# A graph layer on one Trainium2 core: ScalarE fetches some chunks of edges by columns, and the division moves from VectorE's selections to ScalarE's row copies

## The chip, the cores and the metric

The kernel runs on one core of a Trainium2 chip. The metric is the time of one execution on the device in microseconds; lower is better. A core has TensorE (PE in the profile), VectorE (DVE), ScalarE (ACT), GpSimd (POOL) and the queue engine SyncE (SP), each with its own stream of instructions, and 16 DMA engines that move data between the chip's memory and the core's on-chip memories. An engine runs its instructions in their order; what passes between engines goes by semaphores.

## What is computed

A graph of 12500 nodes and 200000 edges, sorted by destination, with 128 features to a node. Two layers of aggregation over the edges stand between a layer norm and a residual sum. Cut to what matters:

```python
h = maximum(layernorm(x), 0)
w = edge_weight / maximum(segment_sum(edge_weight, dst), EPS)[dst]
feat = relu(h @ W_pool + b_pool)
neigh = segment_max(feat[src] * w[:, None], dst)
rst = h @ W1_self + neigh @ W1_neigh + b1
h1 = relu(rst / maximum(norm(rst), EPS))
neigh2 = segment_sum(h1[src] * w[:, None], dst) / maximum(deg, 1)[:, None]
out = x + relu(h1 @ W2_self + neigh2 @ W2_neigh + b2)
```

The costly parts are the two gathers by `src`, 200000 rows of 512 bytes each, and the two reductions by `dst`, a maximum in layer 1 and a sum in layer 2.

## The kernel before

Edges go in **groups** of 512, 391 of them in each layer, and a group in four **chunks** of 128. For a chunk, `gather` (L525) has POOL issue one indirect DMA that fetches 128 rows of a table in memory by a list of sources, one row to a partition: `feat_d` in layer 1, `h_d` in layer 2. So a group has four such gathers, into one buffer of a ring (`gt`; 11 buffers in layer 2, up to 18 in layer 1).

There is a second way to get a chunk. The tables also lie in on-chip memory, transposed: a node is a column of 128 values (`one_way`, `other_way`). The class `Columns` has an engine copy a chunk column by column, at addresses that it reads into registers. `load` has SP bring the list of 128 addresses; `places_of` (L766) reads 16 of them at a time into the engine's registers (a `TENSOR_LOAD`, which the engine's sequencer does); `fetch` copies the 16 columns of this **burst**. Eight bursts make a chunk. What `Columns` is given decides which groups take part: the chunk `j`, the `first` group and `every`, the distance between them. Its `plan` spreads the eight bursts over the turns ahead of the group: in layer 1 they begin some `every` turns before and end one turn before the group, in layer 2 the span is at most five turns and ends four turns before it. In the kernel before DVE alone does this, for chunk 1: in each 8th group of layer 1 from group 33 on, and in each 3rd of layer 2 from group 13 on. It copies two columns with one instruction (`two_by_two`, L813: one changes its sign on the way). For such a chunk `gather` issues nothing.

**Layer 1** (loop from L1064). The order of each engine's instructions is that of the code, turn by turn; a turn `i` issues the gathers of group `i` and works on groups `i-1` to `i-5` at once. PE transposes the gathered chunks into `pm` (L1099); a chunk that came by columns is multiplied with `W_pool` instead (L1006) and cut by ACT (L1011). DVE multiplies by the edges' weights (L1143), runs a scan that carries the maximum along the edges of one destination (L1114), and takes from each pair of edges the value that may end a destination (L1136, L1139, into `sc`). PE turns `sc` so that pairs stand on partitions (`two_pr`, L1156), ACT copies them (`rows`, L1109). DVE builds a selection for them, `sel`: for each pair a row of 48 numbers, one over the sum of the destination's weights (`invT`) at the place of that destination in the group's window and zero elsewhere (L1125, two instructions of 128x48, one of them between the two that make `sc`). PE multiplies `rows` with `sel` (L1165), and ACT copies the window of 48 nodes into the layer's result (L1045). About every 16 turns four tiles of nodes are finished (`quad1`).

**Layer 2** (loop from L1279). DVE builds the selection with weights in two steps, `places` (L1217) and `weighted` (L1222); PE multiplies each chunk with it (`window_product`, L1229); DVE adds the window to the result (`window_add`, L1234). A chunk that came by columns is turned by PE two turns ahead (`turned`, L1204) and copied back to its buffer by ACT (`back`, L804, which also restores the signs by the scale `signs`).

## Time and profile before

| | |
|---|---|
| median of 3 runs | 4603.24 us (4592.86 to 4608.26) |
| profiled execution | 4644.8 us, its span 4643.0 us |
| layer 1, scan of the first to the last group | 168 to 2361 us |
| layer 2, `places` from there on | 2387 to 4625 us |
| indirect DMAs issued by POOL | 2956 |

The times that follow are from the profiled execution. A row of a group reads: line, engine, operation, what it writes and reads, shapes, count, then busy time in us and mean ns of one, then the idle time of the engine just before these instructions and what ended it. In a row of the timeline the start and the time (us) stand first; instructions of one kind in a row are merged, with their count. "issue" is idle time in which the engine waited for nothing that the profile shows.

### The profile page before, as it was taken

To read this page: it belongs to the slowest core of one execution; us is meant where nothing else is said; L and a number is where in the kernel's file an instruction comes from. 1 tells how busy PE (TensorE), PEld (TensorE's weight loads), DVE (VectorE), ACT (ScalarE), POOL (GpSimd) and SP (SyncE) were. 2 spreads that over 40 slices of the span, in tenths; PEclk is the share of its full clock that TensorE was granted. 3 is DMA by queue.
4 is the path that set the end of the run, shared out by engine and by line. 5 is a ranking of instruction groups with operands and counts; after the bars stand their busy time and mean duration, and the time that the engine had idled before them with its cause. 6 is when DMAs were issued, how large, how long until landed. Compare 5 with 4: busy or idle time off the path is not lost.

```text
span 4643.0 us, 42920 instructions
## 1 busy us (share of the span) xinstructions
PE 2052.8 (44%) x8256; PEld 1667.9 (36%) x8256; DVE 3300.0 (71%) x15295; ACT 489.1 (11%) x1472; POOL 2802.4 (60%) x2973
## 2 busy tenths in 40 slices
PE   4564544444445444454433443433333343334334
PEld 3443333333333333333333433333333333333334
DVE  3678887888888888887755666666666666666665
ACT  3531111111111111111110000000000000000000
POOL 5465665666666666666655655565665665655564
PEclk7755555555555555555555555555555555555555
DMA  4343443433444434444421111111111111111111
GB/s 140 119 116 116 124 118 107 118 118 115 122 122 118 118 116 115 118 123 120 116 70 41 43 51 53 46 49 49 49 46 47 51 47 49 48 49 45 49 49 41
DMA packets 189415, 388.81 MB, mean 84 GB/s; under 512 B 58201, under 2 KB 61570, under 8 KB 189140
## 3 DMA queue, kind: packets, MB, share of 16 engines
q0 software_dynamic: 94592, 193.82, 15.3%
q1 hardware_dynamic: 93812, 191.24, 12.8%
q14 instruction: 204, 1.67, 0.1%
q8 instruction: 71, 1.16, 0.1%
q10 hardware_dynamic: 736, 0.92, 0.1%
HBM read 363.91 MB, written 21.87 MB: 83 GB/s over the span
## 4 chain that ended last, share of the span: by engine, by line
DVE 44%; issue 24%; PE 14%; another core or an unknown queue 11%; DVEq 4%; ACT 1%; POOL 1%; DMA 0%; ACTq 0%; POOLq 0%
DVE gt L813 18%; DVE pm L1114 8%; PE pa L1229 7%; DVE pm L1143 4%; DVEq L766 4%; DVE sel L1125 3%; DVE sc L1139 2%; DVE sc L1136 2%; DVE sq L930 1%; PE pm L1099 1%; PE pn L1165 1%; POOL gt L525 1%; DVE place L1217 1%; PE two_pr L1156 1%
## 5 line engine op out<-in xcount | busy, mean ns | idle before, releaser
L813 DVE SCALAR_TENSOR_TENSOR gt<-ends,way 128x2 f32<-128x2 f32 x10560 | 1590.7, 216 | 724.7 <-issue 704.9
L525 POOL DMA_INDIRECT gt<-h_d,srcT x1426 | 1349.9, 947 | 883.2 <-PE pa L1229 409.6
L525 POOL DMA_INDIRECT gt<-feat_d,srcT x1263 | 1197.0, 948 | 668.8 <-issue 337.4
L1229 PE MATMUL pa<-s,gt 128*128 128x24 f32 x3102 | 717.8, 385 | 1268.8 <-issue 1107.8
L1229 PEld LDWEIGHTS pa<-s,gt 128*128 128x128 f32 x3102 | 693.5, 328 | 1349.3 <-issue 1235.9
L1114 DVE TENSOR_TENSOR_SCAN pm<-kt,pm 128x512 f32<-128x512 bf16 x389 | 499.0, 1283 | 27.1 <-issue 26.6
L1156 PE MATMUL two_pr<-near_ones,sc 128*128 128x128 f32 x782 | 244.5, 413 | 531.1 <-ACT rows L1109 290.0
L1099 PE MATMUL pm<-near_ones,gt 128*128 128x128 f32 (+1 forms) x1263 | 319.8, 401 | 349.6 <-issue 242.1
L1099 PEld LDWEIGHTS pm<-near_ones,gt 128*128 128x128 f32 (+1 forms) x1263 | 221.8, 212 | 405.5 <-issue 282.4
L1156 PEld LDWEIGHTS two_pr<-near_ones,sc 128*128 128x128 f32 x782 | 125.0, 202 | 652.4 <-ACT rows L1109 326.7
L1165 PEld LDWEIGHTS pn<-sel,rows 128*128 128x128 f32 x1564 | 354.5, 312 | 0.2
L1165 PE MATMUL pn<-sel,rows 128*128 128x48 f32 x1564 | 338.7, 362 | 0.0
L1125 DVE TENSOR_SCALAR sel<-cols,lastT,invT 128x48 f32<-128x48 f32 x782 | 246.5, 316 | 108.1 <-remote 89.7
L1143 DVE TENSOR_TENSOR pm<-pm,gs 128x512 f32<-128x512 f32 x390 | 269.9, 692 | 68.9 <-remote 32.3
L1109 ACT ACTIVATE rows<-two_pr 128x256 f32<-128x256 f32 x392 | 149.8, 382 | 1205.4 <-remote 701.9
L804 ACT ACTIVATE gt<-flip,ends 128x128 f32<-128x128 f32 x125 | 45.9, 367 | 1746.2 <-PE flip L1204 792.7
L1136 DVE COPY sc<-pm 128x256 f32<-128x256 f32 x391 | 162.5, 416 | 72.1 <-remote 47.1
L1139 DVE COPY_PREDICATED sc<-kt,pm 128x256 f32<-128x256 int16 x389 | 168.4, 433 | 45.0 <-DVE sel L1125 31.3
L525 POOL DMA_INDIRECT w2T<-feat_d,srcT x98 | 92.7, 946 | 88.6 <-DVE raw_mv L539 35.7
L1217 DVE TENSOR_TENSOR place<-place,locT 128x96 f32<-128x96 f32 x391 | 101.6, 260 | 61.1 <-issue 47.2
L1222 DVE TENSOR_TENSOR s<-place,w2T 128x96 f32<-128x96 f32 x391 | 97.8, 250 | 27.2 <-issue 26.3
L1234 DVE TENSOR_TENSOR way<-pa,way 128x41 f32 x391 | 75.6, 193 | 54.7 <-PE pa L1229 22.6
(305 smaller groups left out, 1963.4 us busy)
## 6 DMA issues: line engine op xcount, KB each, us to landing
gs<-in_edge_weight SPq DMA_DIRECT2D x389, 256.0 KB
kt<-keep_d SPq DMA_DIRECT2D x97, 512.0 KB
gt<-h_d,srcT POOLq DMA_INDIRECT x1426
gt<-feat_d,srcT POOLq DMA_INDIRECT x1263
feat_d<-fr SPq DMA_DIRECT2D x24, 256.0 KB
xr<-in_x SPq DMA_DIRECT2D x24, 256.0 KB
out<-o SPq DMA_DIRECT2D x24, 256.0 KB
h_d<-sq SPq DMA_DIRECT2D x23, 256.0 KB
```

Of the source, the lines that this page charges most:

```text
L525: nc.gpsimd.indirect_dma_start(out=gt[:k, j, :], out_offset=None, in_=table_d[:, :], in_offset=bass.IndirectOffsetOnAxis(ap=srcT[:k, t, j, ...
L766: _, self.held[g, r] = nc.values_load_multi_w_load_instructions(self.lists[self.place[g]][:, r:r + BURST], [self.engine], min_val=self.at, ...
L813: nc.vector.scalar_tensor_tensor(slot[:, r + e:r + e + 2], zero_high, columns_read[e], columns_read[e + 1].to_broadcast([P, 2]), op0=OP.su ...
L1099: nc.tensor.transpose(pms[i][:, j * P:j * P + k], gt[:k, j, :], ident[:k, :k])
L1114: nc.vector.tensor_tensor_scan(pm[:, :ne], kt[:, :ne], pm[:, :ne], carry, op0=OP.add, op1=OP.max)
L1125: nc.vector.tensor_scalar(part, cols[:k, 1, :], lastT[:k, t, j, r:r + 1], invT[:k, t, j, r:r + 1], op0=OP.is_equal, op1=OP.mult)
L1136: nc.vector.tensor_copy(sc[:, :ne // 2], two[:, :, 1])
L1139: nc.vector.copy_predicated(sc[:, :ne // 2], new[:, :, 1], two[:, :, 0])
L1143: nc.vector.tensor_tensor(pms[i][:, :n], rows[:, :n], ws.pop(i)[:, :n], OP.mult)
L1156: nc.tensor.transpose(prs[g][:k, j, :], sc[:, j * P:j * P + k], ident)
L1165: nc.tensor.matmul(pas[g], rows[:k, j, :], sel[:k, j, :], start=j == 0, stop=j == len(chunks) - 1)
L1229: nc.tensor.matmul(pas[g][:, PART_AT[j]:PART_AT[j] + PART], gt[:k, j, :], s[:k, j, :], start=j == len(chunks) - 1, stop=j == 0, skip_group ...
```

## The change

A second `Columns` is added in each layer, for ACT and chunk 2: each 4.25th group of layer 1 from group 30 on (the group is 30 plus the whole part of a multiple of 4.25), each 3.5th of layer 2 from group 14 on. ACT copies one column with one instruction (`one_by_one`, by `by_scalar`, L804), with the sign as it is. These are 85 chunks in layer 1 and 107 in layer 2; POOL issues 192 indirect DMAs less. In layer 1 the multiplication and the cut follow as for DVE's chunks, the cut in one instruction; in layer 2 the turn by PE and the copy back by ACT, with no scale.

The selection becomes one instruction of 128x96 on DVE that writes one or zero; the division is done by ACT in the row copies, which become two of 128x128 with `invT` as their scale.

```diff
--- before.py
+++ after.py
@@ -997,7 +997,8 @@
 
         pms, scs, sels, prs, rws, pas = ({} for _ in range(6))
         bycol = []
-        for k, engine, copy, j, every, first in ((0, mybir.EngineType.DVE, two_by_two, 1, 8, FIRST + 16),):
+        for k, engine, copy, j, every, first in ((0, mybir.EngineType.DVE, two_by_two, 1, 8, FIRST + 16),
+                                                 (1, mybir.EngineType.Activation, one_by_one, 2, 4.25, FIRST + 13)):
 
             def slot(g, j=j):
                 return buffer(g, True)[:, j, :]
@@ -1105,36 +1106,33 @@
                 t, r, ne, chunks = pairs_of(g)
                 rws[g] = wk.tile([P, Q // 2, D], F32, name="rows", bufs=2)
                 pr = prs.pop(g)
-                for j, k in (((slice(0, Q // 2), P),) if ne == G else chunks):
-                    nc.scalar.activation(rws[g][:k, j, :], pr[:k, j, :], AF.Copy)
+                for j, k in chunks:
+                    nc.scalar.activation(rws[g][:k, j, :], pr[:k, j, :], AF.Copy, scale=invT[:k, t, j, r:r + 1])
             g = due(1)
             if g is not None:
                 ne = edges_of(g)[2]
                 kt, pm = kts.pop(g), pms.pop(g)
                 nc.vector.tensor_tensor_scan(pm[:, :ne], kt[:, :ne], pm[:, :ne], carry,
                                              op0=OP.add, op1=OP.max)
-            picks = []
-            if due(3) is not None:
-                t, r, _, chunks = pairs_of(due(3))
+
+            def pick():
+                t, r, ne, chunks = pairs_of(due(3))
+                n, k = len(chunks), chunks[-1][1]
                 sel = sels[due(3)] = wk.tile([P, Q // 2, LW], F32, name="sel", bufs=2)
-                picks = [(sel[:k, j, :], k, t, j, r) for j, k in chunks]
-
-            def pick():
-                if picks:
-                    part, k, t, j, r = picks.pop(0)
-                    nc.vector.tensor_scalar(part, cols[:k, 1, :], lastT[:k, t, j, r:r + 1],
-                                            invT[:k, t, j, r:r + 1], op0=OP.is_equal, op1=OP.mult)
+                for a, b, k in ((0, n, P),) if ne == G else [(j, j + 1, k) for j, k in chunks]:
+                    nc.vector.tensor_tensor(sel[:k, a:b, :], cols[:k, 1:2, :].to_broadcast([k, b - a, LW]),
+                                            lastT[:k, t, a:b, r:r + 1].to_broadcast([k, b - a, LW]), OP.is_equal)
 
             for c in bycol[:1]:
                 c.ahead()
-            pick()
+            if due(3) is not None:
+                pick()
             if g is not None:
                 carry = pm[:, ne - 1:ne]
                 sc = scs[g] = wk.tile([P, G // 2], F32, name="sc", bufs=2)
                 two = pm[:, :ne].rearrange("p (c two) -> p c two", two=2)
                 new = kt[:, :ne].bitcast(I16).rearrange("p (c two) -> p c two", two=2)
                 nc.vector.tensor_copy(sc[:, :ne // 2], two[:, :, 1])
-            pick()
             if g is not None:
                 nc.vector.copy_predicated(sc[:, :ne // 2], new[:, :, 1], two[:, :, 0])
             if i < NG:
@@ -1195,7 +1193,8 @@
             nc.vector.tensor_copy(iota[:, j, :], cols[:, 0, at:at + PART])
 
         bycol = []
-        for k, engine, copy, j, every, first in ((0, mybir.EngineType.DVE, two_by_two, 1, 3, 13),):
+        for k, engine, copy, j, every, first in ((0, mybir.EngineType.DVE, two_by_two, 1, 3, 13),
+                                                 (1, mybir.EngineType.Activation, one_by_one, 2, 3.5, 14)):
 
             def slot(g, j=j):
                 return buffer(g, False)[:, j, :]
```

Three places show what this does to the order. First ACT in layer 1, two turns in a row, before; `way` is the layer's result, `pn` the product with the selection:

```order
L1109 ACTIVATE rows<-two_pr 128x256
L1045 ISA
L1045 ACTIVATE way_66<-pn 128x48
L1109 ACTIVATE rows<-two_pr 128x256
L1045 ISA
L1045 ACTIVATE way_66<-pn 128x48
```

And two turns in which it fetches, now (`listed` are the lists of addresses, `way_65` the table, `gt` the buffer):

```order
L804 ACTIVATE gt_102<-way_65 128x1 x16
L766 TENSOR_LOAD listed
L804 ACTIVATE gt_102<-way_65 128x1 x16
L766 TENSOR_LOAD listed
L1110 ACTIVATE rows<-two_pr,invT 128x128 x2
L1046 ISA
L1046 ACTIVATE way_66<-pn 128x48
L804 ACTIVATE gt_102<-way_65 128x1 x16
L766 TENSOR_LOAD listed
L804 ACTIVATE gt_102<-way_65 128x1 x16
L766 TENSOR_LOAD listed
L1110 ACTIVATE rows<-two_pr,invT 128x128 x2
```

Between a turn's row copies and the next there are now two bursts of 16 copies with their loads, and the row copy is in two parts.

Second DVE in layer 1, around the selection, before (its own burst of columns at the end of a turn, the scan, the load for the next burst):

```order
L813 SCALAR_TENSOR_TENSOR gt_107<-ends,way_65 128x2 x8
L1114 SCALAR_TENSOR_TENSOR pm<-kt,pm 128x512
L766 TENSOR_LOAD listed
L1125 TENSOR_SCALAR sel<-cols,lastT,invT 128x48
L1136 COPY sc<-pm 128x256
L1125 TENSOR_SCALAR sel<-cols,lastT,invT 128x48
L1139 COPY_PREDICATED sc<-kt,pm 128x256
L1143 TENSOR_TENSOR pm<-pm,gs 128x512
```

and now:

```order
L813 SCALAR_TENSOR_TENSOR gt_106<-ends,way_65 128x2 x8
L1115 SCALAR_TENSOR_TENSOR pm<-kt,pm 128x512
L766 TENSOR_LOAD listed
L1123 TENSOR_TENSOR sel<-cols,lastT 128x96
L1135 COPY sc<-pm 128x256
L1137 COPY_PREDICATED sc<-kt,pm 128x256
L1141 TENSOR_TENSOR pm<-pm,gs 128x512
```

One instruction is gone, and the two that make `sc` follow each other directly.

Third ACT in layer 2. Before, it had only the copies back from `flip` (and one copy for every four tiles of nodes):

```order
L804 ACTIVATE gt_101<-flip,ends 128x128
L804 ACTIVATE gt_104<-flip,ends 128x128
L804 ACTIVATE gt_107<-flip,ends 128x128
L946 ACTIVATE oT_43860<-pn,b_col 128x512
L804 ACTIVATE gt_99<-flip,ends 128x128
```

Now there are bursts between them, in most turns two, in some three:

```order
L804 ACTIVATE gt_99<-way_66 128x1 x16
L766 TENSOR_LOAD listed
L804 ACTIVATE gt_103<-way_66 128x1 x16
L766 TENSOR_LOAD listed
L804 ACTIVATE gt_107<-flip,ends 128x128
L804 ACTIVATE gt_107<-flip 128x128
L804 ACTIVATE gt_103<-way_66 128x1 x16
L766 TENSOR_LOAD listed
L804 ACTIVATE gt_103<-way_66 128x1 x16
L766 TENSOR_LOAD listed
```

The copy back with `ends` is that of DVE's chunk, the one without that of ACT's own; both stand behind the bursts that were issued before them.

## Prediction

> **What bounds the kernel now.** I read the shares and the chain of waits on the page first.
>
> ```profile
> span 4643.0 us, 42920 instructions
> PE 2052.8 (44%) x8256; PEld 1667.9 (36%) x8256; DVE 3300.0 (71%) x15295; ACT 489.1 (11%) x1472; POOL 2802.4 (60%) x2973
> DVE 44%; issue 24%; PE 14%; another core or an unknown queue 11%; DVEq 4%; ACT 1%; POOL 1%; DMA 0%; ACTq 0%; POOLq 0%
> ```
>
> DVE is the busiest engine and leads the chain; ACT, which the change loads, is busy for 11%. Averages over two layers say little, so I took a stretch of 1800 us from each by the view of windows: all engines (first two rows), then the scan of L1114, once a group of layer 1, then `places` (L1217), once a group of layer 2.
>
> ```profile
> 500.00:2300.00 1800.00, 857.51 (x3512) 668.58 (x3512) 1468.99 (x4741) 246.46 (x838) 1159.55 (x1225) 0.55 0.40 118
> 2600.00:4400.00 1800.00, 712.63 (x2816) 612.82 (x2816) 1171.18 (x7622) 51.80 (x125) 1080.40 (x1143) 0.50 0.17 48
> 500.00:2300.00 1800.00, 409.57 (x319) 0.55 0.40 118
> 2600.00:4400.00 1800.00, 81.59 (x314) 0.50 0.17 48
> ```
>
> The columns are PE, PEld, DVE, ACT and POOL. A group takes 1800/319 = **5.64 us in layer 1** and 1800/314 = **5.73 us in layer 2**. DVE is busy 4.60 us of a group in layer 1 and 3.73 in layer 2. Where the rest of layer 2 goes stands in the groups by line of the same stretch:
>
> ```profile
> L525 POOL DMA_INDIRECT gt<-h_d,srcT x1143 | 1081.5, 946 | 722.8 <-PE pa L1229 360.2 <-issue 315.7 <-remote 27.1
> L813 DVE SCALAR_TENSOR_TENSOR gt<-ends,way 128x2 f32<-128x2 f32 x6654 | 1012.4, 216 | 527.4 <-issue 510.2
> L1217 DVE TENSOR_TENSOR place<-place,locT 128x96 f32<-128x96 f32 x314 | 81.6, 260 | 49.1 <-issue 38.4 <-DVE way L1234 10.5
> ```
>
> Before L813, the column fetch, DVE stood idle for 527 us, 1.68 us a group, and waited for nobody: "issue". POOL's largest wait is for PE, that is, for a buffer to come free. So layer 2 is held by DVE and not by the gathers. But the timeline shows that the two are tied:
>
> ```profile
> 3187.11 0.94 POOL L525 DMA_INDIRECT gt<-h_d,srcT  x1 [2.56 <-PE pa L1229]
> ...
> 3204.62 0.95 POOL L525 DMA_INDIRECT gt<-h_d,srcT  x1 [0.30 <-issue]
> 3210.67 0.95 POOL L525 DMA_INDIRECT gt<-h_d,srcT  x1 [5.11 <-PE pa L1229]
> 3211.92 0.95 POOL L525 DMA_INDIRECT gt<-h_d,srcT  x1 [0.30 <-issue]
> ```
>
> ```profile
> 3197.78 0.48 DVE L813 SCALAR_TENSOR_TENSOR gt<-ends,way 128x2 f32<-128x2 f32 x3 [1.07 <-issue]
> ...
> 3204.16 0.22 DVE L813 SCALAR_TENSOR_TENSOR gt<-ends,way 128x2 f32<-128x2 f32 x1 [1.07 <-issue]
> ...
> 3215.35 1.17 DVE L813 SCALAR_TENSOR_TENSOR gt<-ends,way 128x2 f32<-128x2 f32 x8 [0.17 <-issue]
> ...
> 3216.82 1.14 DVE L813 SCALAR_TENSOR_TENSOR gt<-ends,way 128x2 f32<-128x2 f32 x8
> ```
>
> Between 3187.11 and 3204.62 the gathers follow each other at 1.25 us without a pause. After some ten microseconds of that, DVE starts one or a few pairs of columns between gaps of about 1.1 us, and goes back to bursts of eight once POOL has run out of buffers. In a good stretch a burst takes 3216.82 − 3215.35 = **1.47 us**; over the 1800 us it took (1012.4 + 527.4)/6654 × 8 = **1.85 us**, 1.26 times as much. At 1.47 a group of layer 2 would need 8 × 1.47/3 = 3.92 us of DVE for columns and (1171.18 − 1012.4)/314 = 0.51 for the rest, 4.4 in all. POOL needs (4 − 1/3) × 1.25 = 4.58. The two are about equally fast, and POOL, whenever DVE falls behind, runs ahead until its buffers are full.
>
> In layer 1 POOL needs (4 − 1/8) × 1.25 = 4.84 of 5.64 us, and DVE's 4.60 carries the chain together with waits that the profile can't name.
>
> **The change, part by part.** *One selection.* In layer 1 DVE now does this in each group:
>
> ```profile
> 1206.45 0.28 DVE L1125 TENSOR_SCALAR sel<-cols,lastT,invT 128x48 f32<-128x48 f32 x1
> 1206.65 0.41 DVE L1136 COPY sc<-pm 128x256 f32<-128x256 f32 x1
> 1206.98 0.37 DVE L1125 TENSOR_SCALAR sel<-cols,lastT,invT 128x48 f32<-128x48 f32 x1
> 1207.20 0.43 DVE L1139 COPY_PREDICATED sc<-kt,pm 128x256 f32<-128x256 int16 x1
> 1207.53 0.69 DVE L1143 TENSOR_TENSOR pm<-pm,gs 128x512 f32<-128x512 f32 x1
> ```
>
> From the first selection to the predicated copy it is 0.75 us. The single selection of 128x96 has no row; L1217, of that size and kind, takes 0.260, some 0.17 of it before the next can start. The copy then takes 0.33 (its step to the second selection now) to 0.41 (if the predicated copy must wait for its end). So 0.50 to 0.58 remain, and 0.17 to 0.25 us a group go; I take 0.17. For 391 groups that is 66 us of DVE's time.
>
> *The division goes to ACT.* One row copy becomes two with a scale that is read from SBUF. What ACT's instructions cost, by the groups (rows 1 to 3 and 5), the timeline (row 4) and the view of one line (row 6):
>
> ```profile
> L1109 ACT ACTIVATE rows<-two_pr 128x256 f32<-128x256 f32 x392 | 149.8, 382 | 1205.4 <-remote 701.9 <-PE pn L1165 203.2 <-issue 189.9
> L1045 ACT ACTIVATE way<-pn 128x48 f32 x391 | 81.6, 209 | 129.6 <-issue 66.1 <-PE pn L911 41.5 <-PE pn L1165 7.7
> L804 ACT ACTIVATE gt<-flip,ends 128x128 f32<-128x128 f32 x125 | 45.9, 367 | 1746.2 <-PE flip L1204 792.7 <-PE pa L1229 569.2 <-remote 199.6
> 245.61 1.63 ACT L555 ACTIVATE lastT<-lastT,raw_off,raw_rstd 128x128 f32<-128x128 f32 x4
> L555 ACT ACTIVATE lastT<-lastT,raw_off,raw_rstd 128x128 f32<-128x128 f32 x4 | 1.6, 481 | 0.0
> L766 DVEq TENSOR_LOAD <-listed x1360: 1093/1099/1684, 315.6 to 4605.1; - x195
> ```
>
> 256 and 48 columns differ by 173 ns, 0.83 ns a column, so an ACT copy with plain scale starts from 169 ns. Four copies of 481 ns in a row take 1.63 us: each starts 383 ns after the last, an overlap of 98. L804 has one scale from SBUF: 367 − 98 = 0.27 us a step. Two such against one of 0.28 add 0.26 us a group to ACT.
>
> *ScalarE's columns.* 85 chunks in layer 1 and 107 in layer 2 are now copied column by column: 128 copies of 128x1 and eight loads of 16 addresses each. No row has such a copy. From below it is 169 + 1 − 98 = 72 ns a step, all loads hidden: 1.15 us a burst of 16. From above, DVE's step for its pairs, (1.14 − 0.216)/7 = 132 ns, and the load, which holds the sequencer for 1.10 us (the last row above), not hidden at all: 3.2 us. L555 reads SBUF and not PSUM: 481 less 107 for its columns and 2 × 92 for its two operands from SBUF (92 = 367 − 107 − 168) is 190, a step of 93 ns. That is the value I take. In DVE's burst of 1.47 us, eight steps of 132 leave 0.42 of the load's 1.10 open, so about five queued instructions cover the rest; five of ACT's cover 0.47 and leave 0.63. A burst is then 16 × 0.093 + 0.63 = **2.12 us** and a chunk 17.0.
>
> ACT in a group: layer 1 has 246.46/319 = 0.77 now, 0.26 for the rows, 0.06 for the chunk's relu, 17.0/4.25 = 4.00: **5.1 us**. Layer 2 has 51.80/314 = 0.17, 0.08 for the copy back, 17.0/3.5 = 4.86: **5.1 us**. Both lie a tenth under today's group, and ACT becomes the fullest engine of both layers. It isn't free: behind each burst wait the row copies and the window copy of layer 1, and DVE's chunk, coming back from its flip, in layer 2; PE waits for these and DVE for PE.
>
> *The gathers.* 192 of 2956 fall away: POOL needs (4 − 1/8 − 1/4.25) × 1.25 = 4.55 in layer 1 and (4 − 1/3 − 1/3.5) × 1.25 = 4.23 in layer 2. SP has 192 more short loads of lists in its queue, half a KB each, two buffers to a list, loaded two turns ahead of use; PE has 107 more flips of 0.45 us in layer 2, where it is idle most of the time. I cost both at nothing. That holds as long as ACT keeps up: a late ACT keeps a list's buffer, and the weights of layer 1 queue behind it on SP.
>
> **The sum.** POOL, at 4.23 against 5.1, will now wait a little in most groups of layer 2 instead of running for 18 us without a pause, and it is after such runs that DVE's gaps came. So I expect a group to approach its fullest engine, ACT with 5.1, and leave a third of the distance for waits: 5.30 in layer 1, 5.25 in layer 2. Columns are fetched from turn 25 to 390 and from 7 to 383: 365 × 0.34 + 376 × 0.48 = 124 + 181 = **305 us**. DVE's 66 us are in it. The profiled execution took 4644.8 us (span 4643.0), 0.9% above the median of the runs, 4603.24; the same gain gives **4298 us**.
>
> **A rule against it.** DVE's gaps look like a port that is taken. The Trainium skill, "SBUF — State Buffer", section "Who interferes with whom", has VectorE and GpSimd share one pair of ports: a VectorE instruction with two SBUF inputs, as L813 is, fully blocks against a GpSimd instruction that reads SBUF; ScalarE waits for nobody. The row at 3215.35 speaks against it: eight pairs at full step while gathers follow at 1.25 us. By the rule each gather removed would give DVE its share of the gaps and no more, the second rival's price.
>
> **Rivals.**
>
> 1. *ACT too slow* (the other side). If ACT's bursts stretch as DVE's do, by 1.26, a burst is 2.67 us, a chunk 21.4, and ACT needs 6.13 in layer 1 and 6.35 in layer 2: +0.49 × 365 + 0.62 × 376 = +412, 5015 us. It decides from a burst of 2.4 us on, in both layers: (5.64 − 1.1) × 4.25/8 and (5.73 − 0.25) × 3.5/8. For it: 2.12 is near 2.4, and DVE's gaps have no cause that leaves ACT out. Against: it needs columns that are slow on ACT, of which no row tells. With the upper bound of 3.2 it would be +1200.
> 2. *A share for each gather.* 527 us of gaps at 1143 gathers are 0.46 us a gather; 192 fewer give 88, with DVE's 66 a gain of 154: 4449 us. For it: gaps and gathers come together. Against: at the row of 3215.35 they don't.
> 3. *DVE stays the bound.* POOL waited for buffers already; if fewer gathers change nothing in DVE's gaps, only the selection counts: 4537 us.
> 4. *ACT just eats what DVE gains*: 4603 us.
>
> **How the numbers follow.** Forecast 0.49 (4150 to 4440), rival 1 0.25, rival 2 0.10, rival 3 0.11, rival 4 0.05. Faster by over 0.3% (14 us, about what a measurement can tell here) is 0.49 + 0.10 + 0.11 = 0.70; within 0.05; slower 0.25. The range runs from 4140, layers at 5.1 and a little less, to 4800, which takes in rivals 2 to 4 and half of rival 1; below lie some 0.04, above 0.13.
>
> **What would show it.** L813 on ACT with a step near 93 ns and bursts near 2.1 us; groups of 5.2 to 5.4 us by the scan and by `places`; ACT near 95% busy or in loads; POOL's waits for PE frequent and short; fewer gaps before DVE's L813. A burst over 2.4 us on ACT, or DVE waiting for PE and PE for ACT's rows and flips, would make the prediction wrong on the slow side; unchanged gaps before L813 with POOL waiting longer make rival 3.

## The result, and the profile after

| | before | after |
|---|---|---|
| median | 4600.2 us (4 runs, 4592.86 to 4608.26) | 5248.07 us (4 runs, 5237.06 to 5257.55) |
| profiled execution, its span | 4644.8, 4643.0 us | 5243.78, 5242.0 us |
| layer 1, scan of the first to the last group | 168 to 2361 us | 166 to 2702 us |
| layer 2, `places` from there on | 2387 to 4625 us | 2728 to 5227 us |
| indirect DMAs issued by POOL | 2956 | 2764 |

The ratio is 1.1407 (95% interval 1.1375 to 1.1439): the change makes the kernel **14% slower**, where 4298 us were forecast. Both layers lose, 343 us the first and 261 the second by the table. The runs below went to several chips, and each is set against the kernel before on its own chip, whose time was 4600 to 4656 us on most and 3737 to 3741 on two. One of the slower chips gave 4600.48 us in one series of runs and 4656.38 in a later one, and none was seen in both ranges; so a kind of chip is known here by its time alone. A run given with an interval is the median of 2 to 10 executions, one without is a single execution; the kernel before beside them is a median of 3 to 13 (a single one beside the last run).

The shares and the chain of waits on the page of the changed kernel:

```profile
PE 2034.7 (39%) x8448; PEld 1690.1 (32%) x8448; DVE 3222.4 (61%) x14905; ACT 3256.2 (62%) x26630; POOL 2622.7 (50%) x2781
...
ACT 48%; issue 32%; PE 6%; DVE 5%; ACTq 4%; another core or an unknown queue 3%; POOL 3%; DVEq 0%; DMA 0%; POOLq 0%
```

ACT leads the chain where DVE did, but it is busy for 62%, not 95%, and the second entry of the chain is "issue", time in which an engine waited for nothing that the profile shows. Three groups of the same page show where it lies:

```profile
L804 ACT ACTIVATE gt<-way 128x1 f32 x23168 | 2536.4, 193 | 1457.2 <-issue 1429.3
...
L525 POOL DMA_INDIRECT gt<-h_d,srcT x1319 | 1248.9, 947 | 1243.8 <-PE pa L1228 790.5
L1228 PE MATMUL pa<-s,gt 128*128 128x24 f32 x3102 | 701.5, 373 | 1623.9 <-ACT gt L804 1464.2
```

Before its column copies ACT stood idle for 1457 us, nearly all of it "issue". PE waits for ACT, POOL waits for PE. By the groups of a stretch of 2000 us in each layer (500 to 2500, then 3000 to 5000):

```profile
L804 ACT ACTIVATE gt<-way 128x1 f32 x8425 | 921.1, 196 | 492.2 <-issue 486.6 <-DMA w2T<-feat_d,srcT 0.9
...
L804 ACT ACTIVATE w2T<-way 128x1 f32 x512 | 57.0, 198 | 39.1 <-issue 38.6
```

```profile
L804 ACT ACTIVATE gt<-way 128x1 f32 x11278 | 1232.6, 191 | 691.9 <-issue 686.9
```

Busy and idle time together, a column costs (921.1 + 492.2 + 57.0 + 39.1)/8937 = 169 ns in layer 1 and (1232.6 + 691.9)/11278 = 171 ns in layer 2: bursts of **2.70 and 2.73 us**, above the 2.4 us from which the prediction's first rival decides. DVE in the same two stretches, the rows of its pairs and of the line that runs once a group:

```profile
L1115 DVE TENSOR_TENSOR_SCAN pm<-kt,pm 128x512 f32<-128x512 bf16 x302 | 388.8, 1288 | 0.1
L813 DVE SCALAR_TENSOR_TENSOR gt<-ends,way 128x2 f32<-128x2 f32 x2216 | 314.9, 216 | 1.0 <-issue 1.0
```

```profile
L813 DVE SCALAR_TENSOR_TENSOR gt<-ends,way 128x2 f32<-128x2 f32 x6580 | 985.1, 217 | 506.0 <-issue 490.7
L1216 DVE TENSOR_TENSOR place<-place,locT 128x96 f32<-128x96 f32 x309 | 81.0, 262 | 55.7 <-DVE way L1233 38.2 <-issue 17.3
```

A group takes 2000/302 = **6.62 us** in layer 1 and 2000/309 = **6.47 us** in layer 2 (5.64 and 5.73 before). In layer 1 DVE has no gap before its pairs any more, but it had few before, as this row of the kernel before from 500 to 2300 us shows:

```profile
L813 DVE SCALAR_TENSOR_TENSOR gt<-ends,way 128x2 f32<-128x2 f32 x2376 | 344.5, 213 | 55.3 <-issue 55.2
```

That is 55.3/319 = 0.17 us a group. ACT's gaps in layer 1, (492.2 + 39.1)/302 = 1.76 us a group, are ten times that, so they are more than DVE's gaps handed on. In layer 2 DVE's gaps are what they were, 506.0/6580 = 77 ns a pair against 527.4/6654 = 79, and ACT's came on top.

One such gap from near, in the timeline of layer 2: POOL, then ACT, DVE and PE.

```profile
4100.96 0.94 POOL L525 DMA_INDIRECT gt<-h_d,srcT  x1 [3.44 <-PE pa L1228]
4102.21 0.94 POOL L525 DMA_INDIRECT gt<-h_d,srcT  x1 [0.30 <-issue]
...
4113.46 0.95 POOL L525 DMA_INDIRECT gt<-h_d,srcT  x1 [0.30 <-issue]
```

```profile
4104.39 1.49 ACT L804 ACTIVATE gt<-way 128x1 f32 x15
4106.61 0.30 ACT L804 ACTIVATE gt<-way 128x1 f32 x2 [0.73 <-issue]
4107.33 0.20 ACT L804 ACTIVATE gt<-way 128x1 f32 x1 [0.43 <-issue]
4108.04 0.30 ACT L804 ACTIVATE gt<-way 128x1 f32 x2 [0.50 <-issue]
4108.77 0.20 ACT L804 ACTIVATE gt<-way 128x1 f32 x1 [0.43 <-issue]
4109.49 0.20 ACT L804 ACTIVATE gt<-way 128x1 f32 x1 [0.52 <-issue]
...
4115.15 0.30 ACT L804 ACTIVATE gt<-way 128x1 f32 x2 [1.20 <-issue]
```

```profile
4106.83 1.14 DVE L813 SCALAR_TENSOR_TENSOR gt<-ends,way 128x2 f32<-128x2 f32 x8 [1.00 <-issue]
...
4108.32 1.14 DVE L813 SCALAR_TENSOR_TENSOR gt<-ends,way 128x2 f32<-128x2 f32 x8 [0.17 <-issue]
```

```profile
4120.26 2.33 PE L1228 MATMUL pa<-s,gt 128*128 128x24 f32 x10 [9.02 <-ACT gt L804]
```

POOL begins a run of gathers at 4100.96. ACT still copies 15 columns in 1.49 us, a step of (1.49 − 0.20)/14 = 92 ns, at 4104. From 4106 on it starts one or two columns each 0.7 us, until after the end of the run. DVE goes through full bursts of 1.14 us at the same time. PE then waits 9 us for ACT.

This is the rule and not a chosen case. Call a column copy late if it starts over 0.3 us after the one before it. Counted in the packed trace from 3000 to 5000 us, all 64 runs of gathers at 1.25 us that last 12 us or more have four or more late copies in them or in the 3 us behind them; of the 37 runs that last 3 to 6 us, 8 have. Half of the stretches (four or more late copies, each within 2 us of the next) begin 3.6 to 5.6 us after the first gather of their run.

### The profile page after: what moved, and what is told of

The parts are those of the page before. It is cut to its first block, busy times and chain, and to the rows that moved or that the text cites. A ratio compares the mean times of both kernels' runs of the same rounds, so it can differ in the third digit from the quotient of the medians.

```text
span 5242.0 us, 69992 instructions
## 1 busy us (share of the span) xinstructions
PE 2034.7 (39%) x8448; PEld 1690.1 (32%) x8448; DVE 3222.4 (61%) x14905; ACT 3256.2 (62%) x26630; POOL 2622.7 (50%) x2781
## 3 DMA queue, kind: packets, MB, share of 16 engines
q14 instruction: 411, 3.37, 0.2%
## 4 chain that ended last, share of the span: by engine, by line
ACT 48%; issue 32%; PE 6%; DVE 5%; ACTq 4%; another core or an unknown queue 3%; POOL 3%; DVEq 0%; DMA 0%; POOLq 0%
ACT gt L804 40%; ACTq L766 3%; ACT rows L1110 3%; POOL gt L525 2%; DVE gt L813 2%; ACT w2T L804 1%; PE pn L910 1%; ACT way L1046 1%; PE pa L1228 1%; PE pm L1100 1%; ACT pm L1012 1%; PE pn L911 1%; PE pn L1163 1%; PE two_pr L1154 1%
## 5 line engine op out<-in xcount | busy, mean ns | idle before, releaser
L804 ACT ACTIVATE gt<-way 128x1 f32 x23168 | 2536.4, 193 | 1457.2 <-issue 1429.3
L813 DVE SCALAR_TENSOR_TENSOR gt<-ends,way 128x2 f32<-128x2 f32 x10560 | 1563.5, 217 | 645.1 <-issue 626.0
L525 POOL DMA_INDIRECT gt<-h_d,srcT x1319 | 1248.9, 947 | 1243.8 <-PE pa L1228 790.5
L525 POOL DMA_INDIRECT gt<-feat_d,srcT x1189 | 1128.5, 949 | 1045.0 <-PE pm L1100 676.2
L1228 PE MATMUL pa<-s,gt 128*128 128x24 f32 x3102 | 701.5, 373 | 1623.9 <-ACT gt L804 1464.2
L1100 PE MATMUL pm<-near_ones,gt 128*128 128x128 f32 x1189 | 314.1, 411 | 272.3 <-ACT pm L1012 247.2
L1123 DVE TENSOR_TENSOR sel<-cols,lastT 128x96 f32<-128x96 f32 x392 | 97.0, 248 | 426.1 <-PE pn L1163 370.9
L1100 PEld LDWEIGHTS pm<-near_ones,gt 128*128 128x128 f32 x1189 | 231.4, 232 | 319.9 <-ACT pm L1012 275.9
L1110 ACT ACTIVATE rows<-two_pr,invT 128x128 f32<-128x128 f32 x782 | 245.9, 364 | 68.0 <-issue 38.8
L1046 ACT ACTIVATE way<-pn 128x48 f32 x391 | 84.0, 215 | 103.8 <-PE pn L911 71.2
```

Source lines behind the costliest of these rows:

```text
L525: nc.gpsimd.indirect_dma_start(out=gt[:k, j, :], out_offset=None, in_=table_d[:, :], in_offset=bass.IndirectOffsetOnAxis(ap=srcT[:k, t, j, ...
L804: nc.scalar.activation(out, in_, AF.Copy, **scale)
L813: nc.vector.scalar_tensor_tensor(slot[:, r + e:r + e + 2], zero_high, columns_read[e], columns_read[e + 1].to_broadcast([P, 2]), op0=OP.su ...
L1100: nc.tensor.transpose(pms[i][:, j * P:j * P + k], gt[:k, j, :], ident[:k, :k])
L1110: nc.scalar.activation(rws[g][:k, j, :], pr[:k, j, :], AF.Copy, scale=invT[:k, t, j, r:r + 1])
L1228: nc.tensor.matmul(pas[g][:, PART_AT[j]:PART_AT[j] + PART], gt[:k, j, :], s[:k, j, :], start=j == len(chunks) - 1, stop=j == 0, skip_group ...
```

## Experiments

My theory after this: instructions of ACT and DVE **start late while gathers are in flight**; ACT needs 16 starts for a burst where DVE needs 8, and so it becomes what ends last. The rival: the columns cost ACT too much in any case, or their loads and code hold it up. (Code here is the stream of instructions that an engine is fed.)

### Parts of the change

`e1_sel`, no columns on ACT in either layer (the selection and the row copies alone); `e2_act1`, ACT's columns in layer 1 only; `e3_act2`, in layer 2 only. From the changed kernel:

```diff
-        for k, engine, copy, j, every, first in ((0, mybir.EngineType.DVE, two_by_two, 1, 8, FIRST + 16),
-                                                 (1, mybir.EngineType.Activation, one_by_one, 2, 4.25, FIRST + 13)):
+        for k, engine, copy, j, every, first in ((0, mybir.EngineType.DVE, two_by_two, 1, 8, FIRST + 16),):
...
-        for k, engine, copy, j, every, first in ((0, mybir.EngineType.DVE, two_by_two, 1, 3, 13),
-                                                 (1, mybir.EngineType.Activation, one_by_one, 2, 3.5, 14)):
+        for k, engine, copy, j, every, first in ((0, mybir.EngineType.DVE, two_by_two, 1, 3, 13),):
```

(both for `e1_sel`, the second for `e2_act1`, the first for `e3_act2`). `e5_nogather` is the changed kernel without the gathers of layer 2 from group 200 on; PE there multiplies old rows:

```diff
-                gts[i] = gather(buffer(i, False), h_d, i, besides=bycol)
+                gts[i] = gather(buffer(i, False), h_d, i, besides=bycol) if i < 200 else buffer(i, False)
```

> The kernel before with the one selection and ACT's two scaled row copies alone; no columns on ACT. Theory A (ACT's stream of columns is what costs the time; the selection is a small gain on DVE): layer 1 goes from 5.64 to about 5.47 us a group, layer 2 stays at 5.73, 4530 to 4590 us in all. Theory B (the selection, or the second row copy on ACT, costs part of the loss): layer 1 over 5.7 us a group, over 4620 us.

> The change without ACT's columns in layer 2. Theory A: layer 1 as in the change, 6.6 us a group, layer 2 back at 5.73, about 4950 us. A rival, that the longer program as such slows both layers: layer 2 stays over 6 us a group.

> The change without ACT's columns in layer 1. Theory A: layer 1 at about 5.5 us a group, layer 2 as in the change, 6.5, about 4850 us.

> The change, with all gathers of layer 2 left out from group 200 on (PE works on what the buffers hold from earlier groups); columns on DVE and ACT as before. Theory A1 (ACT's and DVE's starts are slowed while gathers are in flight): from group 200 on no stretches with steps of 0.7 us, ACT's bursts at 1.9 us throughout, a group at 8 x 1.9 / 3.5 + 0.25 = 4.6 us; the first 200 groups as in the change, 6.5. Theory A2 (the instructions themselves come too slowly, whatever POOL does): the stretches stay and a group stays over 6 us. Theory A3 (the loads of addresses): the same as A2, bursts over 2.4 us.

All four ran on a chip where the kernel before took 3737.32 us: 3744.78 (ratio 1.0017, 1.0007 to 1.0027), 3724.46, 3616.26 and 3591.4 us. Three rows of their pages, `e1_sel` first, then two of `e3_act2`:

```profile
L813 DVE SCALAR_TENSOR_TENSOR gt<-ends,way 128x2 f32<-128x2 f32 x10560 | 1519.7, 215 | 239.9 <-issue 217.9
```

```profile
L813 DVE SCALAR_TENSOR_TENSOR gt<-ends,way 128x2 f32<-128x2 f32 x10560 | 1520.8, 215 | 206.9 <-issue 183.3
L804 ACT ACTIVATE gt<-way 128x1 f32 x13696 | 1361.1, 188 | 38.9 <-issue 17.6 <-PE pa L1227 16.2 <-ACT gt L804 1.1
```

Here DVE's gaps are a third (240 us, not 725), and ACT has next to none: (1361.1 + 38.9)/13696 = 102 ns a column, bursts of 1.64 us. And here the columns **gain**: those of layer 2, with the one selection that alone was worth nothing, make 3.2% (3616.26 against 3737.32). `e5_nogather` couldn't test the gathers, since there was no gap before group 200 to take away. Its first 200 groups of layer 2, which are the changed kernel's own, took 4.25 us each, and those without gathers, from 2850 to 3550 us, 700/165 = 4.24.

So I ran both kernels again, unchanged: does the loss go with the chip?

> The change as it is, once more, beside the kernel before. In the four runs just made no stretch of slow starts is left, in kernels with and without ACT's columns. Theory S (the change loses only where instructions start slowly while gathers are in flight, and gains where they don't): without such stretches layer 1 at 4.6 us a group and layer 2 at 4.25, about 3595 us beside 3737, ratio 0.96; with them 5245 beside 4600, ratio 1.14. Theory T (the change loses anyway, the two layers' columns together): slower than before, whatever the stretches.

> The kernel before as it is, for its trace beside that of the change. Theory S: without slow stretches DVE's bursts of columns at 1.47 us throughout, layer 1 at 4.7 and layer 2 at 4.55 us a group, 3737 us; with them 5.64 and 5.73, 4600 us.

This chip was one of the others: 5316.49 us against 4647.38 (1.1454, 1.1427 to 1.1481) and 4647.69 for the kernel before, taken as a run of its own. The loss is there again. There is no run of the whole changed kernel on a chip of the quicker kind; what it would do there rests on its parts.

### What the gathers have to do with it

Four kernels on one chip with the kernel before at 4600.48 us: the changed kernel, the one without gathers from group 200 on, one with narrow gathers there and one with pauses of POOL there. The last two:

```diff
+            nc.gpsimd.indirect_dma_start(
+                out=gt[:k, j, :16], out_offset=None, in_=table_d.rearrange("n (a b) -> (n a) b", b=16)[:, :],
+                in_offset=bass.IndirectOffsetOnAxis(ap=srcT[:k, t, j, r:r + 1], axis=0))
```

```diff
+    idle = rp.tile([P, 2], F32, name="idle")
...
+            if j % 2:
+                for _ in range(4):
+                    nc.gpsimd.memset(idle, 0.0)
             nc.gpsimd.indirect_dma_start(
```

> The changed kernel as it is. Theory S: what it does hangs on whether ACT and DVE get into stretches in which instructions start only every 0.7 us while gathers are in flight. If groups of layer 2 show such stretches here, they last 6.2 to 6.8 us and the run is 5200 to 5350, 13 to 15% above before on the same chip; if there are none (steps of ACT's columns over 0.3 us are under a tenth of their time), groups are 4.2 to 4.6 us and the run is 3570 to 3640, 3 to 5% below before. Theory T (the columns on ACT cost more than they free in any case): above before either way.

> The changed kernel without the gathers of layer 2 from group 200 on (their buffers keep old rows, so the output of these nodes isn't the reference's); what ACT and DVE fetch by columns stays. If the stretches of late starts come from gathers in flight (theory G): groups before 200 as in the changed kernel of the same chip (6.2 to 6.8 us where there are stretches), from 200 on 4.2 to 4.7 us, with hardly a step of ACT's columns over 0.3 us. If they come from the engines' own instruction streams (theory I: ACT's 16 loads and 16 copies a burst, fetched code): 6.0 to 6.8 us on both sides of group 200. On a chip without stretches: 4.2 to 4.3 on both sides, and nothing is told apart.

> The changed kernel with gathers of 16 instead of 128 elements a row in layer 2 from group 200 on (an eighth of the bytes, the same number of gathers and of rows; the rest of each chunk keeps old values, so the output of these nodes isn't the reference's). Theory G1 (what the gathers write, the bytes into SBUF, holds starts back): groups from 200 on fall to 4.2 to 4.8 us. Theory G2 (what POOL does to issue them, once for each row, holds starts back): they stay at 6.0 to 6.8 us where those before 200 are there. Without stretches on this chip: 4.2 to 4.4 on both sides.

> The changed kernel with four small memsets (about 0.5 us by 118 ns each) on POOL ahead of each second gather of layer 2 from group 200 on, so that POOL never issues more than two gathers without a pause; POOL then needs about 5.2 us a group (3.38 gathers of 1.25 us and two pauses). Theory R (stretches come after a long run of gathers without a pause, as runs of 12 to 15 us always had one and runs of 3 to 6 us had one in seven): groups from 200 on fall to 5.2 to 5.6 us. Theory N (only the mean number of gathers in a time counts): they stay at 6.2 to 6.8 us. Without stretches: 4.2 before 200, about 5.2 behind it.

Measured: 5253.37 us (1.1417, 1.1334 to 1.1501), 4818.73, 5253.27 and 5056.55. In the stretch from 4100 to 4750 us, which lies behind group 200 in all four, the groups by line give for ACT's copies, in the order above:

```profile
L804 ACT ACTIVATE gt<-way 128x1 f32 x3651 | 397.8, 190 | 229.3 <-issue 227.6 <-DVE gt L813 0.4
```

```profile
L804 ACT ACTIVATE gt<-way 128x1 f32 x5596 | 556.6, 188 | 7.5 <-issue 5.5
```

```profile
L814 ACT ACTIVATE gt<-way 128x1 f32 x3648 | 398.0, 190 | 230.2 <-issue 228.9
```

```profile
L819 ACT ACTIVATE gt<-way 128x1 f32 x4325 | 471.2, 189 | 148.1 <-issue 141.6 <-ACT gt L819 0.5
```

And for `places`, once a group, the first, second and fourth:

```profile
L1216 DVE TENSOR_TENSOR place<-place,locT 128x96 f32<-128x96 f32 x100 | 26.0, 260 | 15.8 <-DVE way L1233 11.1 <-issue 4.7
```

```profile
L1216 DVE TENSOR_TENSOR place<-place,locT 128x96 f32<-128x96 f32 x154 | 40.3, 262 | 24.6 <-DVE way L1233 23.6 <-issue 1.0
```

```profile
L1231 DVE TENSOR_TENSOR place<-place,locT 128x96 f32<-128x96 f32 x119 | 31.0, 261 | 19.5 <-DVE way L1248 13.0 <-issue 6.5
```

Without gathers the idle time before ACT's copies falls from 229 us to 7.5, a column costs (556.6 + 7.5)/5596 = 101 ns, and a group goes from 650/100 = 6.5 us to 650/154 = **4.22 us**. Ahead of group 200 the same execution, `s_nogather` from 3000 to 3900 us, is like the changed kernel:

```profile
L804 ACT ACTIVATE gt<-way 128x1 f32 x5050 | 552.2, 190 | 313.7 <-issue 310.0 <-ACT gt L804 0.2
L1216 DVE TENSOR_TENSOR place<-place,locT 128x96 f32<-128x96 f32 x140 | 36.4, 260 | 25.8 <-DVE way L1233 18.8 <-issue 6.8
```

There a column costs (552.2 + 313.7)/5050 = 171 ns and a group takes 900/140 = 6.43 us. The loads, the copies and the code of ACT are the same on both sides of group 200, so by themselves they don't hold it up. With gathers of an eighth of the bytes nothing changes at all (3648 copies, 230.2 us): it is not the bytes but something that a gather of 128 rows brings with it at either width. With the pauses the idle time falls to 148 us and the group to 650/119 = 5.46 us. POOL got more gathers through than without pauses:

```profile
L525 POOL DMA_INDIRECT gt<-h_d,srcT x338 | 319.8, 946 | 334.9 <-PE pa L1228 245.0 <-issue 88.3 <-PE flip L1203 0.9
```

```profile
L541 POOL DMA_INDIRECT gt<-h_d,srcT x403 | 381.7, 947 | 154.5 <-issue 76.0 <-PE pa L1243 49.0 <-ACT gt L819 6.0
```

403 gathers against 338 in the same 650 us, with fewer late starts: it isn't the mean number of gathers that counts, but how they follow one another. On the quicker kind of chip that isn't enough either: in `e3_act2` POOL's gathers of layer 2 follow each other at 1.25 us nearly throughout (95% of the steps from 2100 to 3500 us are at most 1.26), and ACT has the 38.9 us of gaps shown above.

The packets in the traces tell where no delay is seen. `e1_sel`, from 2100 to 3500 us, and `v_sel` below, from 2700 to 4400, are the same kernel on the two kinds of chip. On both, 95% of the gathers have their first packet within 1.67 us of the issue, and the last packet of 95% ends within 2.53 us in the first and 2.42 in the second: the gathers are no slower where ACT and DVE start late, and no queue of them builds up. The other suspect is the code, which a DMA queue of its own brings ("q14 instruction" on the page of the changed kernel: 411 packets, 3.37 MB, nearly all of 8 KB). A packet of it takes 0.40 us at the median and never over 0.97, and none is under way from 4104.90 to 4122.91 us, where the stretch shown above lies. So late code isn't seen either, though nothing here excludes a delay behind that queue.

### Is it a bound, and is the rest of the change free?

On a chip with the kernel before at 4649.7 us: the pauses in both layers of the changed kernel; the same in the kernel before; the changed kernel with half of ACT's chunks; and the selection alone once more.

```diff
-                                                 (1, mybir.EngineType.Activation, one_by_one, 2, 4.25, FIRST + 13)):
+                                                 (1, mybir.EngineType.Activation, one_by_one, 2, 8.5, FIRST + 13)):
...
-                                                 (1, mybir.EngineType.Activation, one_by_one, 2, 3.5, 14)):
+                                                 (1, mybir.EngineType.Activation, one_by_one, 2, 7, 14)):
```

> The changed kernel with the pauses (four memsets of POOL, 0.43 us, ahead of each second gather) in both layers from their first gathered group on. If starts are held back after long runs of gathers (theory R; the pause took layer 2 from 6.5 to 5.45 us a group), layer 1 falls too, to 5.4 to 5.9 us by POOL's 3.64 gathers of 1.25 and two pauses, and the run is 4420 to 4620 where before has 4600: about as fast as before or up to 4% faster. If layer 1's loss has another cause than layer 2's: layer 1 stays at 6.6 us, the run at 4800 to 4900. Where a chip shows no stretches: 3950 to 4200, above the 3595 that the changed kernel should have there.

> The kernel before with the same pauses in both layers. POOL then needs about 5.5 us a group in layer 1 (3.88 gathers) and 5.3 in layer 2 (3.67). Theory R: DVE's late starts shrink, groups 5.4 to 5.7 us, the run 4430 to 4620. If pauses only help where ACT is what ends last: groups 5.8 to 6.3, the run 4700 to 4950.

> The changed kernel with half of ACT's chunks (each 8.5th group of layer 1, each 7th of layer 2). If what the change loses is that ACT's bursts of 2.8 us end last (theory L: bursts of a chunk of 22.5 us in 3.5 groups make 6.4 us a group), ACT has 3.2 us a group and is no longer last: groups 5.5 to 5.8 us, the run 4480 to 4660, near before. If the columns lose by something that each of them adds (theory E: half the columns, half the loss): groups 6.0 to 6.2, the run 4880 to 4960.

> The kernel before with one selection a group and the dividing row copies alone, no columns on ACT. Where there are stretches of late starts: 4540 to 4640 (my term: 66 us less on DVE, of which late starts may leave nothing; on another chip, without stretches, it was 1.0017 of before). If the selection itself loses where there are stretches: over 4700.

`v_half` took 4673.16 us, 0.5% above before. Half of the columns would have lost some 320 us if each cost its share; they lost 23. So the loss is a **bound**: ACT's late bursts end last when there are enough of them (ACT's share of the chain is 12% here and 48% in the full change). ACT's late starts are still there, but it also waits for PE, which the full change hardly knew:

```profile
L804 ACT ACTIVATE gt<-way 128x1 f32 x11648 | 1331.2, 194 | 1569.2 <-issue 1118.3 <-PE pa L1228 411.7 <-remote 16.6
```

`v_sel` took 4647.97 us, the same as before. Its rows, and the same two of before behind them:

```profile
L813 DVE SCALAR_TENSOR_TENSOR gt<-ends,way 128x2 f32<-128x2 f32 x10560 | 1588.7, 216 | 704.5 <-issue 683.4 <-DMA gt<-h_d,srcT 0.5
...
L1122 DVE TENSOR_TENSOR sel<-cols,lastT 128x96 f32<-128x96 f32 x392 | 94.7, 242 | 165.9 <-remote 146.7 <-issue 16.0 <-PE pn L1162 2.6
```

```profile
L813 DVE SCALAR_TENSOR_TENSOR gt<-ends,way 128x2 f32<-128x2 f32 x10560 | 1590.7, 216 | 724.7 <-issue 704.9
...
L1125 DVE TENSOR_SCALAR sel<-cols,lastT,invT 128x48 f32<-128x48 f32 x782 | 246.5, 316 | 108.1 <-remote 89.7 <-issue 11.9 <-PE pn L1165 2.0
```

The selection takes 242 ns (the prediction took 260), DVE is busy for 3224.1 us instead of 3300.0, and it waits longer in front of the selection, mostly for what the profile can't name ("remote").

`v_pboth` took 4732.52 us (1.0192, 1.0157 to 1.0227), more than the 4420 to 4620 expected: layer 1 is at 1900/318 = 5.97 us a group by the count of its scans, layer 2 at 2000/348 = 5.75. The pauses give back 0.65 of 0.98 us a group in layer 1 and 0.72 of 0.74 in layer 2, which speaks for one cause in both; a run without gathers, which would show it for layer 1, was not made. ACT still leads the chain, with 59%, and its copies are still late, in layer 1 (500 to 2400 us) and in layer 2 (2700 to 4700):

```profile
L819 ACT ACTIVATE gt<-way 128x1 f32 x8921 | 979.1, 194 | 340.1 <-issue 329.2 <-DVE sc L1152 1.1
```

```profile
L819 ACT ACTIVATE gt<-way 128x1 f32 x12649 | 1387.0, 189 | 519.8 <-issue 502.4 <-ACT gt L819 1.3 <-DVE place L1231 1.0
```

That is 148 and 151 ns a column, bursts of 2.37 and 2.41 us. `v_pbefore`, the kernel **before** with the same pauses, took 4495.28 us, 3.3% less than before. DVE's gaps more than halved, from 724.7 us:

```profile
L828 DVE SCALAR_TENSOR_TENSOR gt<-ends,way 128x2 f32<-128x2 f32 x10560 | 1519.6, 215 | 329.0 <-issue 307.1
```

POOL then leads the chain, with 59%, where DVE did before: with the pauses the gathers have become the bound.

### Pauses, and a version that beats both

> The kernel before with four memsets on POOL ahead of each second gather, again and timed in rounds (one look gave 4495 against 4650, a ratio of 0.967). Theory R: 0.955 to 0.98 on a chip with stretches; 1.0 to 1.04 on one without.

> The changed kernel with half of ACT's chunks and the pauses in both layers. Half alone was 4673 (1.005 of before), the pauses alone took the whole change from 1.14 to 1.02 and before to 0.967. If the two add up (ACT isn't last with half of its chunks, POOL has fewer gathers to issue: 3.76 in layer 1, 3.52 in layer 2, with pauses 5.6 and 5.3 us): groups 5.3 to 5.5, the run 4380 to 4490, a ratio of 0.94 to 0.965, the fastest of all. If ACT's late starts keep them from it: 0.98 to 1.01.

> The kernel before with two memsets (about 0.22 us) on POOL ahead of each gather but the first of a group, in place of four ahead of each second one: less pause in all (0.65 instead of 0.86 us a group), but none longer than 0.22 us. If a run is ended by any pause (theory R1): as fast as with the longer ones or faster, 4430 to 4530. If a pause must be long enough for the gathers in flight to drain (theory R2; one lands 2.1 us after its issue, so that more of them stay in flight here): 4540 to 4660, nearer to before.

On a chip with before at 4656.38 us: `w_pbefore` 4497.96 (0.9649, 0.9624 to 0.9675), so the gain holds. `w_phalf`, half of ACT's chunks with the pauses in both layers, **4389.97 us (0.9417, 0.9392 to 0.9441)**, the fastest on such chips. Its groups of layer 2, from 2500 to 4200 us:

```profile
L1231 DVE TENSOR_TENSOR place<-place,locT 128x96 f32<-128x96 f32 x324 | 84.6, 261 | 71.2 <-issue 36.7 <-DVE way L1248 34.4
```

1700/324 = 5.25 us. POOL in the same stretch:

```profile
L541 POOL DMA_INDIRECT gt<-h_d,srcT x1123 | 1066.9, 950 | 321.7 <-issue 244.5 <-ACT gt L819 8.1 <-PE pa L1243 3.7
...
L540 POOL MEMSET idle<- 128x2 f32 x2125 | 221.6, 104 | 92.1
```

2125 memsets are 531 pauses, 1.64 a group and not the two of the expectations, since a chunk that comes by columns has no pause. POOL's own sum is (4 − 1/3 − 1/7) × 1.25 and 1.64 pauses of 0.42 us, 5.09. It hardly waits for ACT (8.1 us) or PE (3.7), so POOL is the bound of layer 2 now; over the whole kernel it leads the chain with 29%. `w_spread` took 4610.77 us. Its short pauses were meant to tell the length of a pause from the length of a run. The timelines of POOL, in `s_pause` and in `w_spread`, show why they don't:

```profile
4400.39 0.94 POOL L541 DMA_INDIRECT gt<-h_d,srcT  x1 [0.30 <-issue]
4401.33 0.59 POOL L540 MEMSET idle<- 128x2 f32 x4
4402.06 0.95 POOL L541 DMA_INDIRECT gt<-h_d,srcT  x1
```

```profile
3400.58 0.95 POOL L541 DMA_INDIRECT gt<-h_d,srcT  x1
3401.53 0.27 POOL L540 MEMSET idle<- 128x2 f32 x2
3401.95 0.95 POOL L541 DMA_INDIRECT gt<-h_d,srcT  x1
```

Four memsets lengthen the step of 1.25 us to 1.67, two only to 1.37, since the 0.30 us between gathers hides most of them. By the counts of memsets (4228 in `w_spread`, 5408 in `w_pbefore`) that is 2114 pauses of 0.12 us, 0.32 us a group, against 1352 of 0.42, 0.73 a group. The last run was to mend that, with three:

```diff
-            if j % 2:
-                for _ in range(4):
+            if j:
+                for _ in range(3):
                     nc.gpsimd.memset(idle, 0.0)
```

> The kernel before with three memsets on POOL ahead of each gather but the first of a group. In the traces two memsets added only 0.11 us to the step of 1.25 us between gathers and four added 0.42, so that the spread pauses of the run before made 0.33 us a group in all and the long ones 0.84; three should add about 0.26 to 0.28, 0.8 a group. If it is the rate of a run of gathers that matters (theory R3: the mean step in a run, 1.46 us with the long pauses, about 1.45 here): 4470 to 4530, as with the long ones. If a pause has to be long for the backlog to drain (theory R2): 4560 to 4650. On a chip without late starts it tells nothing.

It came to a chip with before at 3740.57 us and took 4453.82: it says nothing of late starts. It does say that on such a chip pauses cost 19%, because there POOL was the bound already (`e1_sel`'s chain begins with POOL, 31%). With pauses both kinds of chip take nearly the same time, 4497.96 us (`w_pbefore`) and 4453.82, and in both POOL leads the chain with 60%. **Length of a pause or rate of a run stays open.**

## Why the prediction was wrong

- **What bounded the kernel.** Right in that DVE's gaps before its pairs held layer 2 and that they came with runs of gathers. The experiment without gathers shows that the gaps need the gathers for ACT; for DVE the pauses in the kernel before point the same way.
- **The step that failed** is the first sentence of the sum: that POOL "will now wait a little in most groups of layer 2 instead of running for 18 us without a pause", and that the gaps would shrink with that. POOL waits in long pieces and then runs again (the row at 4100.96: a wait of 3.44 us, then eleven gathers without a pause). DVE's gaps in layer 2 stayed at 77 ns a pair, and ACT got gaps of its own, which the sum had as none.
- **ACT's burst**, the term that carried this: 2.12 us forecast, 2.70 and 2.73 measured. The step of 93 ns was right (92 at 4104.39), and without gathers a burst takes 16 × 0.101 = 1.61 us, less than forecast: 16 steps of 93 ns leave 0.12 us open for the load, not 0.63. What the term lacked is the late starts. Put into the prediction's own account the measured columns give 1.09 + 128 × 0.169/4.25 = 6.18 us of ACT for a group of layer 1 and 0.25 + 128 × 0.171/3.5 = 6.50 for layer 2. Measured were 6.62 and 6.47: layer 2 is ACT alone, layer 1 has 0.4 us of waits besides. A slip of the sum's own is small: a third of the distance makes 5.27 and 5.31 us a group, some 292 us of gain in place of 305.
- **Rival 1** described what happened, with its threshold (2.4 us), its reason (gaps "have no cause that leaves ACT out") and nearly its burst (2.67). It had a chance of 0.25, and the range was cut through its middle. The case against it, that no row told of slow columns on ACT, was no evidence: ACT had no columns to be slow with.
- **One selection.** The size was about right (248 ns in the changed kernel; DVE busy for 75.9 us less in `v_sel`, where 66 were forecast), the worth was not: it gave nothing on either kind of chip (1.0017 on one, 4647.97 against 4649.7 on another), since DVE waits longer instead.
- **Row copies**: 364 ns against the 367 supposed; small, and no part of the loss, by `v_sel`.
- **Gathers**: POOL's 192 fewer gathers were worth nothing where ACT was last, as its idle time before those of layer 2 rose from 883.2 to 1243.8 us. On the other kind of chip they are the gain: from 2100 to 3500 us a group of layer 2 goes from 1400/306 = 4.58 us in `e1_sel`, POOL's sum, to 1400/328 = 4.27 in `e3_act2`. There POOL no longer decides, though its sum of (4 − 1/3 − 2/7) × 1.25 = 4.23 is near: DVE leads the chain with 50%, and the groups without any gather in `e5_nogather` take 4.24.
- **The rule on the ports.** The Trainium skill, "SBUF — State Buffer", section "Who interferes with whom", says that PE and ACT never wait for anyone at the ports. Here ACT starts late for 10 us while DVE, the engine that by that section shares a port with GpSimd, runs full bursts (4106.83 and 4108.32), and gathers with an eighth of the bytes change nothing. So, as far as that section goes, what delays ACT's starts is not that port, and the rule gives no reason to think ACT safe from it.

What stays open is what differs between the two kinds of chip, which step of a gather (what POOL does for it, or the DMA engines' work) delays the other engines, and what in those engines is held up.

## What to carry to other kernels

Idle time "issue" on one engine can be a symptom with a cause outside of it, as it was here: before work is moved to another engine, ask whether the cause goes with it, and price the new engine with the same stretch until a run shows otherwise. ACT, with 16 starts a burst, paid for late starts most here, and it mattered only from the point where it ended last: half of ACT's columns cost 0.5% where all of them lose 14%. Check which engine bounds the kernel on more than one chip: some 0.7 to 0.8 us of pauses a group gained 3.5% on one and lost 19% on another.

## What was not expected of the hardware

- The same kernel takes 3737 to 3741 us on two chips and 4600 to 4656 us on the others, repeatably in a series of runs: 13 runs within 3734.26 to 3741.27, 7 within 4651.29 to 4674.51. In layer 2 the difference lies in late starts: between `e1_sel` and `v_sel`, the same kernel, the layer goes from 1763 to 2240 us and the gaps before DVE's pairs in it from 239.9 to 673.4. Layer 1 goes from 1825 to 2195 us with 31.1 us of such gaps, and that part stays open.
- Late starts hit one engine while another runs at full step, as at 4106; in layer 1 of the changed kernel DVE has next to none (1.0 us before 2216 pairs) and ACT 1.76 us a group.
- On the slower kind of chip, runs of gathers at 1.25 us are harmless for some microseconds: at 4104, three microseconds into a run, ACT still copied at 92 ns a step, and at 4106.6 no longer. A pause of 0.42 us after every second gather took away a third of ACT's idle time (229 to 148 us), though more gathers were issued.
